# A planner's model of PSUM banks and of some durations, and a new set of its preferences, in a fused attention and feed-forward kernel

## The chip, the cores and the metric

The kernel runs on one core of one Trainium2 chip. The metric is the device time of one execution in microseconds (us), and the median of the runs is what counts. All arithmetic is in 32-bit floats. A core has a matrix engine (TensorE, PE in the profile), VectorE (DVE), ScalarE (ACT), GpSimd (POOL) and a queue that issues DMAs (SP). Matrix products land in PSUM, which has 8 banks of 2 KB in each of its 128 partitions. ACT and DVE read the banks.

## The reference, cut to what matters

Eight sequences `b`, each of 512 rows by 256 columns, go through the same three stages. The function `ffn` is two layers of windowed attention and a gated feed-forward; `ttt` is a sequential update of a matrix, row by row.

```
x = in_x                                      # (8, 512, 256)
x = x + 0.5 * ffn(layernorm(x))               # two layers
x = x + ttt(layernorm(x))
x = x + 0.5 * ffn(layernorm(x))               # the same two layers

ffn, one layer (8 heads of 64, window 128, hidden size 682):
  h = shift_token(x)                          # half of the columns come from the row before
  q, k, v = split(h @ wqkv)
  q, k = rotary(l2norm(q) * qs, l2norm(k) * ks)
  o = softmax(mask(q k^T * 8)) v              # a window sees itself and the one before
  x = x + o @ wo
  a, g = split(layernorm(shift_token(x)) @ w1 + b1)
  x = x + (a * gelu(g)) @ w2 + b2

ttt: z = layernorm(...) ; keys, queries, values = projections of z
  for each row t: y_t = W q_t ; W = W - 0.01 (W k_t - v_t) k_t^T
  result z + y
```

## The kernel before, in words

A sequence is cut into four windows of 128 rows (`NW`). The loops of `sequence` (one for each `b`) run over two halves, two layers, four windows, and in the attention over two groups of four heads. All weights stay in SBUF, so after the first loads the only DMAs are the load of a sequence, a second load of its input, and the store.

The program has no loops on the chip. While it is built, Python makes a list of *nodes*, each a small group of instructions on one engine, with its cost in nanoseconds, the nodes that it depends on, and the buffers that it takes and uses (`Node`, `Val`). `Scheduler.run` then goes through them as a list scheduler: it keeps a modelled clock for each engine, works out for each ready node the time `t` at which it could start, and emits the node with the smallest key. The key is that time, plus the cost of a change (of the shape class on PE, 100 ns; of the activation table on ACT, 1300 ns), minus the node's *preference*: the number of ns in the table `EARLY` under the node's name. A preference of 4700 lets a node go ahead of others whose time is up to 4.7 us earlier. The order in which nodes are emitted is the order of instructions on each engine, and it is all that the planner decides, apart from two choices: a copy out of PSUM may go to ACT or DVE, and some additions and multiplications to DVE or GpSimd. The waits between engines come from the framework, by the tiles that instructions touch, and not from the planner's clock.

Some costs and constants of the model: `HOP` is 60 ns from one engine to the next, `PE_TAIL` 170 ns more after TensorE, `T_TURN` the price of two 64-row transposes, `T_QUAD` and `T_QUADS` those of groups of 64x64 products. A buffer's slot comes free when the last node that uses its `Val` is ready. PSUM is the pool `"ps"` of eight banks; a node that needs a bank takes a `Val("ps")`.

Up to three sequences are in flight (the pool `lane`). `base` and `x` are their residual streams. In the attention of a window, in this order of data:

- `h.turn`, `h.copy` (L542, L506): x is transposed into `hT`.
- `qk` (L594): the products for k, then q, each 512 wide into one bank `pp`. From that bank ACT squares (`qk.square`, L613), and DVE multiplies with the rotary tables twice (`qk.straight` L638, `qk.swapped` L644). `qk.sum` (L620), `qk.add` (L650) and, on GpSimd, `qk.power` (L629, L630) and `k.scale` (L665) follow.
- `v` (L681): the product for v, and `v.copy` (L506).
- `qk.turn` (L704): 16 transposes put rotated k and q into two banks. `both_of` gives a view of both banks at once.
- `qk.copy` (L506), twice: the k half of that view to `kT`, the q half to `qT`, each 512 wide, each on ACT or DVE. Both read the same two banks.
- `sc` (L744): score products of 64x64 blocks from `kT` and `qT`, in two banks, for four heads. It depends on both copies and on `v`'s product.
- `least` (L787, DVE), `exp` (L799, ACT), `recip` (L813, DVE), `shares` (L820, DVE or GpSimd): the softmax.
- `pr.turn` (L846), `pr.copy` (L506), `po` (L883), `po.copy` (L506), `po.add` (L927): the weights are transposed and multiply v.
- `py` (L934), `x.attn` (L943): the output projection, added to x.

The feed-forward takes two windows at a time: `hs` (L972 to L975), `hs.stats`, `hn` (L996), `hn.turn` (L542), `h2T` (L1019), then `gate` and `value` (both L1041), `gelu` (L1063), `g` (L1082), `last` (L1041), `last.gelu` (L1102), `last.g` (L1116), and `down` (L1132), `remains` (L1143), `x.ffn` (L1154). The stage `ttt` solves the row recursion by blocks of 128 rows: products of 64x64 blocks at L1335, and the steps `pred`, `rest`, `u`, `y` (L1488, L1489) and `w` (L1500) window by window.

Nodes on PE have a class (`kind`): "full", "rows" (64-row transposes and others of less than 128 rows), "quad" (64x64 blocks) and "cols". A change of class is what the planner charges with 100 ns.

Of the kernel before, what the change touches and what calls it, by code (L numbers as in the profile page):

```python
# [15 lines left out]
B, S, D = 8, 512, 256  # L16
NW = S // P
HEADS, DH = 8, 64
# [3 lines left out]
NFC = HID // P  # L22
# [62 lines left out]

HOP = 60.0
PE_TAIL = 170.0
T_TURN = 58.0
T_QUAD = 116.0
T_QUADS = 224.0  # L90
T_BLOCKS = 450.0
# [4 lines left out]
def t_mm(n, times=1):  # L96
    return times * 2 * (n * 2 / 2.4 + 2.5)
# [14 lines left out]
def t_pool(n, spread=False):  # L112
# [2 lines left out]


EARLY = {
    "XT": -200,
    "_table": -250,
    "_turn": 250,  # L120
    "base.x": 300,
    "below": 5200,
    "block": 250,
    "bx": 400,
    "bx.copy": 100,
    "bx6": -150,
    "bx6.copy": 800,
    "cross.mask": -650,
    "down": -100,
    "edge": -550,  # L130
    "exp": -950,
    "g": 100,
    "gate": 5950,
    "gram": 250,
    "gram.copy": 2550,
    "h.copy": -250,
    "h.turn": 350,
    "h2T": -900,
    "hn": 250,
    "hn.turn": 250,  # L140
    "hs": 2000,
    "hs.rstd": -800,
    "hs.stats": 300,
    "k.scale": -500,
    "keys": 2350,
    "keys.copy": 500,
    "kq": 3450,
    "kq.copy": -450,
    "last": 400,
    "last.g": 300,  # L150
    "last.gelu": 250,
    "least": -250,
    "ones": -150,
    "po": 2000,
    "po.add": 5000,
    "po.copy": 200,
    "pr.copy": -150,
    "pr.turn": 250,
    "pred": 5000,
    "py": 50,  # L160
    "qk": 150,
    "qk.copy": 50,
    "qk.power": -1000,
    "qk.square": -750,
    "qk.sum": -500,
    "qk.swapped": 4700,
    "qk.turn": 1450,
    "recip": 3000,
    "remains": 1750,
    "rest": 1050,  # L170
    "sc": 4700,
    "start": 3050,
    "tv": 200,
    "tv.add": -1100,
    "u": 100,
    "u.copy": -100,
    "v.copy": 100,
    "value": 150,
    "w": 100,
    "w.add": -500,  # L180
    "x.ffn": -500,
    "x.rstd": -1250,
    "x.scale": 2500,
    "x.stats": -900,
    "xbx": 250,
    "xbx.t": 4750,
    "y": 2850,
    "z.stats": -1150,
    "zT": -1000,
    "zero": -2000,  # L190
    "zn.rstd": -2750,
    "zn.stats": -150,
    "zn.turn": 3000,
}


# [32 lines left out]
class Val:  # L229


    def __init__(self, tag):
        self.tag, self.users, self.slot, self.ap = tag, 0, None, None


class Node:
    def __init__(self, name, prio, eng, cost, emit, deps, takes, uses, kind, tail, port):
        self.name, self.early = name, EARLY.get(name, 0.0) - max(prio[0], 0) * EARLY.get("_seq", 0.0)
        self.prio, self.cost, self.emit, self.takes, self.kind = prio, cost, emit, takes, kind
        self.engs = eng if isinstance(eng, tuple) else (eng,)  # L240
        self.costs = cost if isinstance(cost, tuple) else (cost,)
        self.uses, self.next, self.ready, self.tail, self.port = uses, [], None, tail, port
        self.left = 0
        for d in deps:
            d.next.append(self)
            self.left += 1
        self.deps = deps
        for v in uses:
            v.users += 1


class Scheduler:
# [23 lines left out]
    def run(self):  # L276
        ready = [n for n in self.nodes if n.left == 0]
        left = len(self.nodes)
        while left:
            best = None  # L280
            for n in ready:
                room = self.room(n)
                if room is None:
                    continue
                at = max([room, *(d.ready for d in n.deps)])
                for eng, cost in zip(n.engs, n.costs):
                    t, turn = max(at, self.clock[eng], self.port if eng in n.port else 0.0), 0.0
                    if eng == "PE" and n.kind != self.pe_kind:
                        turn = PE_TURN
                    if eng == "ACT" and n.kind and n.kind != self.table:  # L290
                        turn = TABLE
                    more = EARLY.get(f"_{'table' if eng == 'ACT' else 'turn'}", 0.0) if turn else 0.0
                    key = (t + turn - n.early + more + (cost if len(n.engs) > 1 else 0.0), n.prio)
                    if best is None or key < best[0]:
                        best = (key, n, eng, cost, t, turn)
            assert best, f"no node can go: {left} left, " + str({k: len(v) for k, v in self.free.items()})
            _, n, eng, cost, t, turn = best
            ready.remove(n)
            left -= 1
            n.ran = eng  # L300
            self.turns[eng] = self.turns.get(eng, 0) + (turn > 0)
            for v in n.takes:
                slots = self.free[v.tag]
                v.slot = min(slots, key=lambda s: s[0])
                slots.remove(v.slot)
                v.ap = v.slot[1]
            n.emit(eng)
            end = self.gate.end(t + turn, cost) if eng == "PE" else t + turn + cost
            self.clock[eng] = end
            if eng in n.port:  # L310
                self.port = end
            if eng == "PE":
                self.pe_kind = n.kind
            if eng == "ACT" and n.kind:
                self.table = n.kind
            n.ready = end + n.tail + (PE_TAIL if eng == "PE" else 0.0)
            for v in n.uses:
                v.users -= 1
                if v.users == 0:
                    v.slot[0] = n.ready  # L320
                    self.free[v.tag].append(v.slot)
            for m in n.next:
                m.left -= 1
                if m.left == 0:
                    ready.append(m)
        return max(self.clock.values())
# [3 lines left out]
def macaron_kernel(ctx: ExitStack, tc: tile.TileContext, a: dict, out: bass.AP):  # L330
# [4 lines left out]
    ps = ctx.enter_context(tc.tile_pool(name="ps", bufs=1, space=bass.MemoryType.PSUM))  # L335
# [147 lines left out]
    def sequence(b):  # L483
# [6 lines left out]
        def pe(name, cost, emit, deps, takes=(), uses=(), kind="full"):  # L490
            return node(name, prio(), "PE", cost, lambda e: emit(), deps, takes, uses, kind)
# [54 lines left out]
        def attention(x, l, ready):  # L546

            wqkv, rt, wo, lnp, w1, b1, w2 = W[l]
            hT, kT, v, laid, vals, done = {}, {}, {}, {}, {}, []
            n_qk = n_v = n_k = None  # L550
            for w in range(NW):

                hT[w], pt = Val("hT"), Val("ps")
                n = transposes(
                    "h.turn",
                    lambda k, pt=pt: pt.ap[:, k * P : (k + 1) * P],
                    lambda k, w=w: x.ap[:, w, k * P : (k + 1) * P],
                    [ready[w], L["ident"]],
                    [pt, hT[w]],
                    [x],  # L560
                    2,
                )
# [11 lines left out]
                else:  # L574
# [7 lines left out]
                        uses=[hT[w], hT[w - 1]],  # L582
# [6 lines left out]
                for i in (1, 0):  # L589
                    pp, rot, tmp, st = Val("ps"), Val("rot"), Val("tmp"), Val("st")  # L590

                    def project(pp=pp, w=w, i=i):
# [14 lines left out]
                        takes=[pp, rot, tmp, st],  # L607
                        uses=[hT[w]],
# [6 lines left out]
                        uses=[pp, tmp],  # L615
# [8 lines left out]
                        uses=[tmp, st],  # L624
# [24 lines left out]
                    def add(e, rot=rot, tmp=tmp):  # L649
# [9 lines left out]
                        uses=[rot, tmp],  # L659
# [37 lines left out]
                def turn(pts=pts, turned=turned):  # L697
                    out = both_of(*pts)
                    for i in (1, 0):
                        rot = turned[i][0].ap  # L700
                        for g in range(HEADS // 2):
# [5 lines left out]

                n_k = pe(
                    "qk.turn",
                    HEADS * T_TURN,  # L710
                    turn,
                    [turned[0][1], turned[1][1], n_k],
                    takes=[*pts, kT[w], qT, oT],
                    uses=[turned[0][0], turned[1][0]],
                    kind="rows",
                )
                made = [
                    copy(
                        "qk.copy",
                        512,  # L720
                        lambda dst=dst: dst.ap.rearrange("p g (r t) -> p r g t", r=2),
                        lambda i=i, pts=pts: both_of(*pts)[:, :, i * 4 * DH : (i + 1) * 4 * DH].rearrange(
                            "p r (g t) -> p r g t", g=4
                        ),
                        [n_k],
# [11 lines left out]
                for g in range(2):  # L737

                    sc, prT = [Val("ps"), Val("ps")], Val("prT")
                    prs, sts = [Val("pr"), Val("pr")], [Val("s8"), Val("s8")]  # L740

                    def scores(sc=sc, g=g, w=w, qT=qT):
# [24 lines left out]

                    n_sc = pe(
                        "sc",
                        2 * (T_QUADS + (T_QUAD if w else 0.0)),  # L770
                        scores,
                        [made[1], n_v, *(laid[j] for j in blocks)],
                        takes=[*sc, *prs, *sts],
                        uses=[qT, *(kT[j] for j in blocks)],
                        kind="quad",
                    )
                    n_w = []
                    for par in range(2):
# [4 lines left out]
                        for k in range(2):  # L783
# [31 lines left out]
                            uses=[st],  # L815
                        )

                        def shares(e, st=st, par=par, prs=prs, nj=nj):
# [13 lines left out]
                                uses=[prs[par], st],  # L832
# [119 lines left out]
        def feed_forward(x, l, ready):  # L952
            wqkv, rt, wo, lnp, w1, b1, w2 = W[l]
            done = []
            for h in range(2):
# [188 lines left out]
                            pys[k].ap[:, 0:D], gT.ap[rows, rem], w2[rows, NFC, :], start=False, stop=True  # L1144
                        )

                n_d = pe("remains", t_mm(D) + 10, remains, [*downs, *made[NFC:]], uses=[*pys, gT], kind="rows")
                for k in range(2):

                    done.append(  # L1150
# [12 lines left out]
        def ttt(base, at):  # L1163
# [285 lines left out]
            for w in range(NW):  # L1449
# [36 lines left out]
                def outputs(w=w, U=U, pyy=pyy):  # L1486
# [3 lines left out]

                n_out = pe(
                    "y",
                    t_mm(D, 2 if w else 1), outputs, [n_uc, n_ca, n_wt], takes=[pyy], uses=[U, va, vb], kind="full"
                )
                if w < NW - 1:
                    pw = Val("ps")
# [160 lines left out]
```

## Time and profile before

| what | value |
|---|---|
| median of 3 runs | 2931.66 us (2930.18 to 2934.65) |
| the profiled execution | 2928.53 us |
| its span, first to last instruction | 2926.8 us |
| TensorE busy, granted clock | 2794.0 us (95%), 0.997 |
| VectorE, ScalarE, GpSimd busy | 1968.5 (67%), 1630.8 (56%), 1294.0 us (44%) |
| chain that ended last | PE 88%, DVE 5%, ACT 4%, POOL 2%, issue 1% |
| DMA | 27.96 MB in all, mean 10 GB/s |

A row of the groups reads: line, engine, operation, output and inputs by the program's names, shape, count; then busy us and mean ns of one; then the idle time of the engine just before these instructions, and what ended most of it. "ps" is any PSUM bank. Weight loads (PEld) overlap the matmuls. In the table of waits a row reads: who waited, for whom, us in total, times, the longest in us. In the timeline: start and length in us, engine, line, operation, count, and in brackets the idle time before it and its releaser.

### The profile page before, as it was taken

How to read it: one execution, taken by the hardware profiler on the slowest of the kernel's cores; microseconds unless marked ns; L12 is line 12 of the kernel's file. 1: busy time of each engine (PE TensorE's matmuls, PEld its weight loads, DVE VectorE, ACT ScalarE, POOL GpSimd, SP SyncE). 2: the span in 40 equal slices, each digit the busy share in tenths (PEclk: the TensorE clock that was granted, in tenths of full speed). 3: DMA queues.
4: the chain of work that ended last, by engine and by line, in shares of the span. 5: the costliest groups of instructions: out<-in, count | busy, mean ns of one | idle time of the engine just before them, and what ended most of it. 6: DMA issues, size and time to landing. Idle time of an engine off the chain costs nothing.

```text
span 2926.8 us, 75703 instructions
## 1 busy us (share of the span) xinstructions
PE 2794.0 (95%) x30448; PEld 2057.5 (70%) x30448; DVE 1968.5 (67%) x6125; ACT 1630.8 (56%) x4328; POOL 1294.0 (44%) x1844
## 2 busy tenths in 40 slices
PE   7999999999999999999999999999999999999997
PEld 4776776776767767677676776767766677676666
DVE  6777666666776666766677666766666666666664
ACT  4655655555566555565555655555455654645553
POOL 5444453544455244452445524454244542444432
PEclk9999999999999999999999999999999999999999
DMA  5000000000000000000000000000000000000000
GB/s 181 2 2 2 2 2 1 2 2 2 23 2 2 2 16 9 2 2 2 20 5 2 2 1 23 2 1 2 1 23 2 2 2 1 16 2 2 9 2 8
DMA packets 20615, 27.96 MB, mean 10 GB/s; under 512 B 2172, under 2 KB 17704, under 8 KB 20264
## 3 DMA queue, kind: packets, MB, share of 16 engines
q1 hardware_dynamic: 20264, 23.12, 2.4%
q8 instruction: 239, 3.92, 0.6%
q14 instruction: 112, 0.92, 0.1%
HBM read 18.93 MB, written 4.19 MB: 8 GB/s over the span
## 4 chain that ended last, share of the span: by engine, by line
PE 88%; DVE 5%; ACT 4%; POOL 2%; issue 1%; DMA 0%; SPq 0%; ACTq 0%; DVEq 0%; POOLq 0%
PE ps L1041 20%; PE ps L594 15%; PE ps L1132 9%; PE ps L934 7%; PE ps L681 7%; PE ps L744 6%; PE ps L883 6%; PE ps L846 4%; PE ps L704 2%; PE ps L542 2%; PE ps L1335 2%; ACT kT L506 1%; PE ps L1143 1%; DVE qT L506 1%; PE ps L972 1%
## 5 line engine op out<-in xcount | busy, mean ns | idle before, releaser
L1041 PE MATMUL ps<-h2T,w 128*128 128x256 f32 (+1 forms) x2816 | 656.1, 383 | 5.0 <-ACT kT L506 2.2
L1041 PEld LDWEIGHTS ps<-h2T,w 128*128 128x128 f32 (+1 forms) x2816 | 520.4, 189 | 109.6 <-issue 21.5
L820 POOL TENSOR_TENSOR pr<-pr,s 128x384 f32<-128x384 f32 (+1 forms) x304 | 240.7, 796 | 649.4 <-DVE s L813 619.3
L594 PE MATMUL ps<-wqkv,hT 128*128 128x512 f32 x1024 | 495.4, 609 | 3.0 <-ACT prT L506 1.3
L799 ACT ACTIVATE pr<-pr,s 128x192 f32<-128x192 f32 (+1 forms) x1024 | 440.5, 433 | 30.7 <-DVE s L787 28.6
L630 POOL TENSOR_TENSOR st<-st,powc 128x8 f32<-128x8 f32 x256 | 433.0, 1691 | 21.3
L787 DVE CUSTOM_DVE_ANT_0 pr<-ps,amask,st 128x192 f32<-128x192 f32 (+1 forms) x1024 | 360.8, 394 | 54.4 <-PE ps L744 52.2
L613 ACT ACTIVATE tmp<-ps 128x512 f32<-128x512 f32 x256 | 153.4, 599 | 290.7 <-DVE rot L638 266.4
L1132 PE MATMUL ps<-w,gT 128*128 128x256 f32 x1280 | 296.6, 382 | 2.1 <-ACT kT L506 1.1
L594 PEld LDWEIGHTS ps<-wqkv,hT 128*128 128x128 f32 x1024 | 184.5, 192 | 152.6 <-issue 136.0
L506 ACT COPY prT<-ps 128x512 f32<-128x512 f32 (+1 forms) x453 | 220.6, 544 | 117.1 <-PE ps L846 106.7
L1132 PEld LDWEIGHTS ps<-w,gT 128*128 128x128 f32 x1280 | 239.6, 190 | 48.0 <-issue 10.0
L744 PE MATMUL ps<-kT,qT 64*64 64x128 f32 (+1 forms) x7168 | 190.8, 251 | 73.5 <-DVE qT L506 37.3
L744 PEld LDWEIGHTS ps<-kT,qT 64*64 64x64 f32 x7168 | 167.6, 133 | 127.2 <-ACT qT L506 55.9
L638 DVE TENSOR_TENSOR rot<-ps,rt 128x512 f32<-128x512 f32 x256 | 175.9, 687 | 120.1 <-PE ps L594 108.8
L934 PE MATMUL ps<-wo,oT 128*128 128x256 f32 x1024 | 243.9, 381 | 0.2 <-DVE oT L927 0.2
L681 PE MATMUL ps<-wqkv,hT 128*128 128x512 f32 x512 | 242.8, 599 | 1.2 <-ACT kT L506 1.2
L629 POOL TENSOR_SCALAR st<-st 128x8 f32<-128x8 f32 x256 | 67.2, 262 | 375.3 <-DVE st L620 371.9
L934 PEld LDWEIGHTS ps<-wo,oT 128*128 128x128 f32 x1024 | 191.6, 190 | 48.4 <-issue 19.9
L883 PEld LDWEIGHTS ps<-prT,v 64*64 64x64 f32 x7168 | 173.8, 133 | 61.7 <-issue 23.0
L1082 DVE SCALAR_TENSOR_TENSOR gT<-ps,b,gl 128x256 f32<-128x256 f32 x320 | 148.7, 481 | 100.2 <-PE ps L1041 59.9
L883 PE MATMUL ps<-prT,v 64*64 64x64 f32 (+1 forms) x7168 | 206.6, 249 | 6.2 <-ACT prT L506 5.3
(127 smaller groups left out, 4488.5 us busy)
## 6 DMA issues: line engine op xcount, KB each, us to landing
x<-in_x_dram SPq DMA_DIRECT2D x8, 512.0 KB, 5.4
base<-in_x_dram SPq DMA_DIRECT2D x8, 512.0 KB, 3.8
out_dram<-base SPq DMA_DIRECT2D x8, 512.0 KB, 3.3
w<-in_w_dram SPq DMA_DIRECT2D x6, 640.0 KB, 8.0
wqkv<-in_wqkv_dram SPq DMA_DIRECT2D x2, 1024.0 KB, 7.2
wqkv<-in_wqkv_dram SPq DMA_DIRECT2D x2, 512.0 KB
wo<-in_wo_dram SPq DMA_DIRECT2D x2, 512.0 KB
gT<-in_rope_dram SPq DMA_DIRECT2D x1, 512.0 KB
```

Of the source, the lines that this page charges most:

```text
L506: (nc.scalar.copy if e == "ACT" else nc.vector.tensor_copy)(dst(), src())
L594: nc.tensor.matmul(pp.ap, hT[w].ap[:, c * P : (c + 1) * P], wqkv[:, c, i * INNER : (i + 1) * INNER], start=(c == 0), stop=(c == 1),)
L630: nc.gpsimd.tensor_tensor(ss, ss, powc[:, 0:HEADS], ALU.pow)
L681: nc.tensor.matmul(pv.ap, hT[w].ap[:, c * P : (c + 1) * P], wqkv[:, c, 2 * INNER : 3 * INNER], start=(c == 0), stop=(c == 1),)
L744: nc.tensor.matmul(sc[par].ap[half(c), k * 4 * DH + at : k * 4 * DH + at + keys.stop - keys.start], qT.ap[half(par), 2 * g + k, half(c)], ...
L787: nc.vector.tensor_tensor_reduce(out=pr(k, nj), in0=sc.ap[:, k * 4 * DH : k * 4 * DH + nj], in1=amask[:, 0:nj] if w else amask[:, 3 * DH : ...
L799: nc.scalar.activation(pr(k, nj), pr(k, nj), AF.Exp, bias=st.ap[:, k : k + 1], scale=-1.0, accum_out=st.ap[:, 2 + k : 3 + k],)
L820: (nc.vector if e == "DVE" else nc.gpsimd).tensor_tensor(both, both, st.ap[:, 4:6].unsqueeze(2).to_broadcast([P, 2, nj]), ALU.mult)
L883: nc.tensor.matmul(po[r].ap[half(par), k * P + first : k * P + first + cols * DH], v[j].ap[half(r), hd * DH : (hd + 1) * DH], prT.ap[half( ...
L934: nc.tensor.matmul(py.ap[:, 0:D], oT.ap[:, c, :], wo[:, c, :], start=(c == 0), stop=(c == INNER // P - 1))
L1041: nc.tensor.matmul(dst.ap[0:rows, 0 : 2 * P], w1[:, kc, col : col + rows], h2T.ap[:, kc, :], start=(kc == 0), stop=(kc == 1),)
L1132: nc.tensor.matmul(py.ap[:, 0:D], gT.ap[:, at : at + P], w2[:, c, :], start=(c == 0), stop=False)
```

## The change

It touches the planner alone: no instruction of the program is added, removed or altered, and only their order can differ, with the choice of engine where there is one. It has three parts.

Banks: each `Val` remembers which engine used it last and until when (`last`). A node that uses a PSUM bank may not start, on the modelled clock, before the last user has ended, if that was on another engine. The rule goes by the banks that a node itself takes or uses.

Durations: `T_TURN` goes from 58 to 62 ns; `qk.turn` gets 50 ns more, `sc` 38, `remains` 94, and `y` 200 where it has two products (w > 0).

Preferences: nearly all of `EARLY` is replaced. Of some 70 entries the lines below show those that the text speaks of and the largest moves.

```diff
-T_TURN = 58.0
+T_TURN = 62.0
...
 EARLY = {
-    "_table": -250,
+    "_table": -500,
     "_turn": 250,
...
-    "below": 5200,
+    "below": -1200,
...
-    "bx6": -150,
+    "bx6": 5050,
...
-    "gate": 5950,
+    "gate": 4800,
...
-    "po": 2000,
-    "po.add": 5000,
+    "po": 3450,
+    "po.add": 500,
...
     "qk.copy": 50,
...
-    "qk.swapped": 4700,
-    "qk.turn": 1450,
+    "qk.swapped": 1600,
+    "qk.turn": 1100,
...
-    "sc": 4700,
-    "start": 3050,
+    "sc": 3850,
+    "start": 5350,
...
+    "v": -50,
...
 class Val:
         self.tag, self.users, self.slot, self.ap = tag, 0, None, None
+        self.last = None
...
 class Node:
+        self.banks = [v for v in self.uses if v.tag == "ps"]
...
 class Scheduler, run:
                     t, turn = max(at, self.clock[eng], self.port if eng in n.port else 0.0), 0.0
+
+                    t = max([t, *(v.last[1] for v in n.banks if v.last and v.last[0] != eng)])
...
             n.ready = end + n.tail + (PE_TAIL if eng == "PE" else 0.0)
+            for v in n.banks:
+                v.last = (eng, n.ready)
...
                 n_k = pe(
                     "qk.turn",
-                    HEADS * T_TURN,
+                    HEADS * T_TURN + 50.0,
...
                         "sc",
-                        2 * (T_QUADS + (T_QUAD if w else 0.0)),
+                        2 * (T_QUADS + (T_QUAD if w else 0.0)) + 38.0,
...
-                n_d = pe("remains", t_mm(D) + 10, remains, [*downs, *made[NFC:]], uses=[*pys, gT], kind="rows")
+                n_d = pe("remains", t_mm(D) + 104.0, remains, [*downs, *made[NFC:]], uses=[*pys, gT], kind="rows")
...
                     "y",
-                    t_mm(D, 2 if w else 1), outputs, [n_uc, n_ca, n_wt], takes=[pyy], uses=[U, va, vb], kind="full"
+                    t_mm(D) if w == 0 else t_mm(D, 2) + 200.0,
+                    outputs, [n_uc, n_ca, n_wt], takes=[pyy], uses=[U, va, vb], kind="full"
```

More of the change, by code (lines that the diff above doesn't have):

```diff
@@ L117 @@
 EARLY = {
-    "XT": -200,
-    "_table": -250,
+    "XT": 400,
+    "XT6": -250,
+    "_table": -500,
     "_turn": 250,
-    "base.x": 300,
-    "below": 5200,
-    "block": 250,
-    "bx": 400,
-    "bx.copy": 100,
-    "bx6": -150,
-    "bx6.copy": 800,
-    "cross.mask": -650,
+    "base.x": 3000,
+    "base.y": -750,
+    "base.z": -1250,
+    "below": -1200,
+    "block": -500,
+    "bx": 450,
+    "bx6": 5050,
+    "cross.mask": 1400,
     "down": -100,
-    "edge": -550,
+    "edge": -50,
@@ L131 @@
     "exp": -950,
     "g": 100,
-    "gate": 5950,
-    "gram": 250,
-    "gram.copy": 2550,
+    "gate": 4800,
+    "gelu": -550,
     "h.copy": -250,
[L137 to L151, printed above, removed]
+    "h.turn": 200,
+    "h2T": -700,
+    "hn.turn": 200,
@@ L152 @@
+    "hs.rstd": -850,
+    "hs.stats": 400,
+    "keys": 1550,
+    "keys.copy": -1000,
+    "kq": 1850,
+    "kq.copy": -500,
+    "last": 1300,
+    "last.g": -200,
+    "last.gelu": 300,
     "least": -250,
-    "ones": -150,
-    "po": 2000,
-    "po.add": 5000,
+    "po": 3450,
+    "po.add": 500,
     "po.copy": 200,
-    "pr.copy": -150,
+    "pr.copy": -100,
     "pr.turn": 250,
-    "pred": 5000,
-    "py": 50,
+    "pred": 3100,
     "qk": 150,
     "qk.copy": 50,
-    "qk.power": -1000,
@@ L164 @@
-    "qk.square": -750,
+    "qk.power": -1250,
+    "qk.square": -600,
     "qk.sum": -500,
-    "qk.swapped": 4700,
-    "qk.turn": 1450,
-    "recip": 3000,
-    "remains": 1750,
-    "rest": 1050,
-    "sc": 4700,
-    "start": 3050,
[L173 to L177, printed above, removed]
-    "value": 150,
[L179 to L186, printed above, removed]
@@ L187 @@
-    "y": 2850,
-    "z.stats": -1150,
-    "zT": -1000,
+    "qk.swapped": 1600,
+    "qk.turn": 1100,
+    "recip": 700,
+    "remains": 1250,
+    "rest": 2800,
+    "sc": 3850,
+    "start": 5350,
+    "tv": 2000,
+    "tv.add": -900,
+    "u.copy": 400,
+    "v": -50,
+    "value": 150,
+    "w.add": -400,
+    "x.attn": -100,
+    "x.ffn": -700,
+    "x.rstd": -1400,
+    "x.scale": 200,
+    "x.stats": 100,
+    "xbx": 1200,
+    "xbx.t": 800,
+    "y": 550,
+    "z.rstd": 1700,
+    "z.scale": 4250,
@@ L190 @@
+    "z.stats": 2350,
+    "zT": -1700,
     "zero": -2000,
-    "zn.rstd": -2750,
-    "zn.stats": -150,
-    "zn.turn": 3000,
+    "zn.rstd": -2850,
+    "zn.scale": 2000,
+    "zn.turn": 4450,
 }
```

## The prediction, made before the result was known

> **What bounds the kernel now.** I read the page first: busy time by engine, then the slices.
>
> ```profile
> span 2926.8 us, 75703 instructions
> PE 2794.0 (95%) x30448; PEld 2057.5 (70%) x30448; DVE 1968.5 (67%) x6125; ACT 1630.8 (56%) x4328; POOL 1294.0 (44%) x1844
> ...
> PEclk9999999999999999999999999999999999999999
> ```
>
> TensorE is at work 95% of the span at full clock; no other engine passes 70%. The change adds and removes no instruction, so it can only take time from the 2926.8 - 2794.0 = 132.8 us in which TensorE stands still, and a little from how its work is ordered. Where those lie, the view by windows tells (length, then PE busy):
>
> ```profile
> 0.00:25.00 25.00, 16.96 (x60) 7.59 (x64) 12.88 (x26) 6.45 (x12) 17.23 (x39) 1.00 0.94 322
> ...
> 100.00:2700.00 2600.00, 2508.34 (x27621) 1857.30 (x27620) 1768.48 (x5519) 1472.38 (x3909) 1167.72 (x1661) 1.00 0.02 5
> ...
> 2850.00:2926.80 76.80, 61.21 (x631) 47.20 (x630) 38.19 (x112) 29.72 (x74) 18.76 (x25) 0.96 0.02 8
> ```
>
> Start (8.0 us) and end (15.6) are the load of the first weights and the dependent chain of the last sequence; no order removes them. 91.7 us lie in the steady middle. Who waits there, from the groups by line (last columns: idle before, releaser) and the table of waits:
>
> ```profile
> L744 PE MATMUL ps<-kT,qT 64*64 64x128 f32 (+1 forms) x7168 | 190.8, 251 | 73.5 <-DVE qT L506 37.3 <-ACT qT L506 35.7 <-ACT hT L506 0.4
> L542 PE MATMUL ps<-sq,x 128*128 128x128 f32 x256 | 48.3, 289 | 18.3 <-DVE x L533 10.0 <-DVE x L1154 4.6 <-DVE tmp L644 2.8
> L883 PE MATMUL ps<-prT,v 64*64 64x64 f32 (+1 forms) x7168 | 206.6, 249 | 6.2 <-ACT prT L506 5.3 <-DVE gT L1116 0.3
> ...
> ACT tmp L613 <- DVE rot L638: 266.4, 203, 3.6
> ...
> DVE qT L506 <- ACT kT L506: 72.0, 49, 3.4
> ```
>
> One place holds 73.5 of it: the score products (L744, node "sc") wait for the copies of q and k out of PSUM (L506, "qk.copy"), in 81 stalls of 0.9 us. The two lower lines are the bank: the DVE copy of qT waits for the ACT copy of kT from the same two banks, and the square on ACT (L613) waits for DVE's product (L638) in the same bank. The timeline shows one stall:
>
> ```profile
> 228.44 0.66 PE L704 MATMUL ps<-sq,rot 64*128 64x64 f32 x16
> ...
> 229.32 0.90 PE L883 MATMUL ps<-prT,v 64*64 64x128 f32 x32 [0.22 <-ACT prT L506]
> 230.29 0.58 ACT L506 COPY kT<-ps 128x512 f32<-128x512 f32 x1 [1.02 <-PE ps L883]
> ...
> 230.90 0.69 DVE L506 COPY qT<-ps 128x512 f32<-128x512 f32 x1 [1.97 <-ACT kT L506]
> ...
> 231.65 1.57 PE L744 MATMUL ps<-kT,qT 64*64 64x128 f32 x64 [1.43 <-DVE qT L506]
> ```
>
> Two delays add up. The copies run one after the other (230.29 to 231.59), which the planner doesn't know. And the first copy starts 1.2 us after its transposes (L704) end at 229.10: it was released by L883, a *later* product that it doesn't read. Pairing the start times of all 128 copy pairs: in 66 the first copy was released by a TensorE instruction later than its transposes, on average 1.0 us (ACT, then DVE) to 1.8 us (both on ACT) after them; these 66 pairs hold 59.3 of the stall. The change doesn't tell the planner of this second delay.
>
> **What the Trainium skill says.** "PSUM — Partial Sum Buffer", section on bank collisions: no two of TensorE, ScalarE and VectorE may touch one bank in the same partitions at once, reads against reads included, and a back end puts a dependency between them. The trace agrees: where ACT copies first and DVE second, DVE starts 33 ns (median) after ACT ends. "Perfetto Trace Analysis", on the most-contended engine, warns that matmul busy time misjudges TensorE, since matmuls are pipelined; so I also take starts: a 128x256 matmul follows another after 216 ns, though its row shows 383. "TensorEngine Tiling (Array Packing)", Key Properties: changing the tiling mode drains TensorE. Here 309 ns instead of 216 pass before a 64x64 product that follows such a matmul, about 93 ns for each of 993 changes of shape class, 92 us. "ScalarE: Activation LUTs", on table loads, gives 1283 ns a load; the trace has 1283.
>
> **The change, part by part**, against the profiled execution (2928.53 us; its span 2926.8 and 1.7 around it). The median of the runs is 2931.66, 3.1 more.
>
> *Bank rule at the copies.* In 55 pairs ACT copies first and DVE second, in 5 the reverse, in 68 both are on ACT. The planner so far takes DVE beside ACT as free: ready after about 0.7 us of copying. With the rule DVE would start behind ACT's 0.59 and one hop and take 0.69, so ACT twice (1.17) is the earlier end, and most pairs go to ACT. By start times and idle in the trace, the 60 mixed pairs hold 39.9 us of the stall and the 68 ACT pairs 33.0, or 0.49 each. If the mixed pairs come to 0.49: 60 x 0.49 = 29, **-11 us**. ACT takes over some 45 copies x 0.59 = 27 us, at 56% busy; DVE loses 31.
>
> *Bank rule at the square.* ACT stands 266.4 us in 203 waits behind L638, with its queue (copies, exps, gelus) behind it. That is no TensorE time in itself, but the planner thinks those followers earlier than they are. With the rule it puts one ahead. In ACT pairs the second copy starts on average 0.7 us after the first has ended, other work being between. I take a third of the 35.7 us that L744 waits for ACT's qT: **-12 us**. Bounds: 0, and all of the 35.7.
>
> *Durations.* qk.turn 8x4+50 = 82 ns x128; pr.turn 16 ns x64 and 32 x192; sc 38 x256; remains 94 x64; y 200 x24: 10.5+7.2+9.7+6.0+4.8 = 38 us of TensorE work that the planner did not count. They agree with the trace (16 transposes of L704 take 553 ns to the next start; 8x58 = 464, new 546). No instruction becomes shorter; the plan of buffers and waits fits better. Idle in the middle outside L744 is 91.7 - 73.5, about 18 us, some of L744's being in the last 227; I take a third, **-6 us**; bounds +10 and -15.
>
> *Preferences.* No direct price. They move whole nodes, and nothing but the first loads, one base reload a sequence and one store waits on a DMA; SP's queue is never what TensorE waits for after 10 us. The penalty for a change of shape class (_turn) stays 250; I take 0, with 5% of 993 x 0.093, 5 us, either way. The penalty for a table load falls from -250 to -500: more of them are possible, see below.
>
> Sum: 2928.5 - 11 - 12 - 6 = 2899.5; plus 3.1: **2903 us**, 1.0% faster. What is late next is the same L744, still 45 us or so, behind copies that wait for later products.
>
> **The rivals.** *B: the stall mostly goes.* The planner sees the copies end half a microsecond later and puts the v product (four matmuls of 429 ns, 1.7 us) between; then even falsely released copies (1.0 to 1.8 us late) are covered. For it: at 95% busy there is always other work of the three sequences in flight. Against: the ACT pairs were already planned serially and still stall. Three quarters of 73.5, 55, less at the same -6 and some hidden drain: 2931.7 - 55 = 2877.
>
> *C: it doesn't do what it says.* The later products are what decides, the copies wait for them as before, and the retuned order brings no more than noise: 2930.
>
> *D: slower, by ACT.* The copies go to ACT and so does a keener change of table. Now there are 78+74+5 = 157 loads of 1.28 us. A load ahead of a copy or an exp delays TensorE by up to 1.28 us, or nothing. With half reaching TensorE, 60 more loads cost 60 x 0.64 = 38; from 29/0.64 = 45 more loads they eat my gain. At 60 with the gain at the square gone too (12): 2903 + 38 + 12 = 2953; as ACT is idle 44% I take it a little milder: 2945.
>
> **How the numbers follow.** My forecast has 0.53, B 0.21, C 0.12, D 0.14. A measurement of this kernel can tell 0.2% (6 us) from no change. Forecast and B are faster; of C a third is faster (0.04) and two thirds the same (0.08); D is slower. So faster 0.78, same 0.08, slower 0.14. My own bounds (square 0 to -35.7, other idle +10 to -15, classes 5) give 2870 to 2931; B's centre is 2877 and its better half reaches 2862; at the top C's 2930 and its noise to 2934. That leaves out D and the best of B, under 2 in 10.
>
> **What would show it.** Right: qT copies on DVE fall from 55 to under 20; the wait of DVE's qT for ACT's kT falls from 72.0 below 25; the wait of the square for L638 falls well below 266.4; L744's idle falls to 40 to 55 us; first copies are still often released by a later product. B is right if L744's idle is below 25. D is right if table loads exceed 200 and PE idle rises at L883 and L846. I am wrong if PE's idle stays at 130 (C), or if the gain comes with PE busy below 2780, which would mean fewer class changes rather than fewer waits.

## The result and the profile after

The changed kernel takes 2897.58 us (median; 2897.02 to 2898.26) where the one before takes 2933.15 beside it. The ratio is 0.9879, 95% interval 0.9862 to 0.9896: 1.2% faster, 35.6 us. Predicted were 2903 us and 28.7 us less. The profiled execution of the kernel before was one of its fastest (2928.53 us), so the two profiles lie only some 30 us apart. Of the reasons that the prediction gave, one holds by itself in a run, and it is worth a third of the gain (11.7 us); most of the rest hangs on a wait that the prediction saw and put aside.

The page of the changed kernel (the lines of its code that the text speaks of are numbered 2 higher than before; busy us by engine):

```profile
span 2896.4 us, 75802 instructions
PE 2792.6 (96%) x30448; PEld 2063.2 (71%) x30448; DVE 1966.6 (68%) x6110; ACT 1638.9 (57%) x4317; POOL 1331.6 (46%) x1884
```

TensorE's busy time has not moved (2794.0 before, a difference of 1.4). Its idle time, span less busy, fell from 132.8 to 103.8 us; 29.0 + 1.4 is the 30.4 by which the span is shorter. From the groups by line, the three places that matter (last columns: idle before, releaser), and from the table of waits the square:

```profile
L746 PE MATMUL ps<-kT,qT 64*64 64x128 f32 (+1 forms) x7168 | 195.6, 255 | 36.4 <-ACT qT L508 32.4 <-DVE qT L508 3.7
L885 PE MATMUL ps<-prT,v 64*64 64x128 f32 (+1 forms) x7168 | 204.5, 249 | 13.0 <-ACT prT L508 9.9 <-DVE prT L508 1.2 <-DVE s L789 1.0
L544 PE MATMUL ps<-sq,x 128*128 128x128 f32 x256 | 46.8, 286 | 10.5 <-DVE x L535 10.5
...
ACT tmp L615 <- DVE rot L640: 162.3, 144, 3.5
```

The scores (L746) stand idle for 36.4 us instead of 73.5, that is 37.1 less; everywhere else together it is 67.4 instead of 59.3, 8 more. And most of the copies of qT that were on DVE have moved to ACT, as the groups by shape show, on ACT, then on DVE:

```profile
L508 ACT COPY qT<-ps 128x512 f32<-128x512 f32 x115 | 67.8, 590 | 64.4 <-PE ps L596 28.6 <-PE ps L1043 10.4 <-DVE row L1469 5.6
L508 ACT COPY kT<-ps 128x512 f32<-128x512 f32 x115 | 67.3, 586 | 236.7 <-PE ps L848 86.7 <-PE ps L706 63.4 <-PE ps L596 38.5
```

```profile
L508 DVE COPY qT<-ps 128x512 f32<-128x512 f32 x13 | 8.9, 688 | 11.3 <-PE ps L885 5.5 <-PE ps L1337 3.3 <-PE ps L1043 1.3
```

Of the q copies 13 are on DVE, 55 before, and DVE's wait for ACT's copy of kT, 72.0 us before, isn't among the first three here: it is under 1.3. But the second line still says what the prediction called a second delay: the copy of kT is released by transposes of other data (L848, 86.7 us) more than by its own (L706, 63.4). Paired by start times (the first copy of a pair is the one that starts earlier), 74 of the 128 first copies are now released by a later product, 66 before, and those pairs hold 31.6 of the 36.4 us. What became of the stall is that the scores come later: the median time from the end of both copies to the start of the scores went from 55 ns, which is no room at all, to 374.

### The profile page after: what moved, and what is told of

It is laid out like the page before. It is cut to its first block, busy times and chain, and to the rows that moved or that the text cites. A ratio compares the mean times of both kernels' runs of the same rounds, so it can differ in the third digit from the quotient of the medians.

```text
span 2896.4 us, 75802 instructions
## 1 busy us (share of the span) xinstructions
PE 2792.6 (96%) x30448; PEld 2063.2 (71%) x30448; DVE 1966.6 (68%) x6110; ACT 1638.9 (57%) x4317; POOL 1331.6 (46%) x1884
## 4 chain that ended last, share of the span: by engine, by line
PE 91%; DVE 3%; ACT 3%; POOL 2%; issue 1%; DMA 0%; SPq 0%; DVEq 0%; POOLq 0%; ACTq 0%
PE ps L1043 21%; PE ps L596 16%; PE ps L1134 9%; PE ps L936 8%; PE ps L683 7%; PE ps L885 6%; PE ps L746 6%; PE ps L848 4%; PE ps L706 2%; PE ps L544 2%; PE ps L1337 2%; PE ps L1145 1%; PE ps L1257 1%; PE ps L974 1%; ACT qT L508 1%
## 5 line engine op out<-in xcount | busy, mean ns | idle before, releaser
L822 POOL TENSOR_TENSOR pr<-pr,s 128x384 f32<-128x384 f32 (+1 forms) x345 | 271.5, 794 | 480.4 <-DVE s L815 476.7
L801 ACT ACTIVATE pr<-pr,s 128x192 f32<-128x192 f32 (+1 forms) x1024 | 441.2, 434 | 57.9 <-DVE s L789 54.4
L615 ACT ACTIVATE tmp<-ps 128x512 f32<-128x512 f32 x256 | 153.1, 598 | 186.9 <-DVE rot L640 162.3
L508 ACT COPY prT<-ps 128x512 f32<-128x512 f32 (+1 forms) x397 | 193.8, 543 | 105.2 <-PE ps L848 99.9
L746 PEld LDWEIGHTS ps<-kT,qT 64*64 64x64 f32 x7168 | 172.1, 136 | 104.5 <-ACT qT L508 58.5
L746 PE MATMUL ps<-kT,qT 64*64 64x128 f32 (+1 forms) x7168 | 195.6, 255 | 36.4 <-ACT qT L508 32.4
L885 PE MATMUL ps<-prT,v 64*64 64x128 f32 (+1 forms) x7168 | 204.5, 249 | 13.0 <-ACT prT L508 9.9
L1065 ACT ACTIVATE gl<-ps,b 128x256 f32<-128x256 f32 x320 | 140.1, 473 | 118.5 <-PE ps L1043 113.1
```

Source lines behind the costliest of these rows:

```text
L508: (nc.scalar.copy if e == "ACT" else nc.vector.tensor_copy)(dst(), src())
L746: nc.tensor.matmul(sc[par].ap[half(c), k * 4 * DH + at : k * 4 * DH + at + keys.stop - keys.start], qT.ap[half(par), 2 * g + k, half(c)], ...
L801: nc.scalar.activation(pr(k, nj), pr(k, nj), AF.Exp, bias=st.ap[:, k : k + 1], scale=-1.0, accum_out=st.ap[:, 2 + k : 3 + k],)
L822: (nc.vector if e == "DVE" else nc.gpsimd).tensor_tensor(both, both, st.ap[:, 4:6].unsqueeze(2).to_broadcast([P, 2, nj]), ALU.mult)
L885: nc.tensor.matmul(po[r].ap[half(par), k * P + first : k * P + first + cols * DH], v[j].ap[half(r), hd * DH : (hd + 1) * DH], prT.ap[half( ...
```

## The experiments

"Close banks" below is the edit that turned out to matter most. The copies read both banks of a pair through one strided view (`both_of`: from the lower bank to the higher, with a step). If the framework takes such a view to touch the banks in between, a copy waits for any product that was emitted earlier into one of these. In the order of the changed program this holds for 75 of the 128 first copies; 74 of them are exactly those that the trace shows released by a later product, and of the other 53 none is. Before, it is 78, of which 66. In the kernel before, where nothing lay between, a first copy began a median of 42 ns after its transposes ended; where something did, 1039.

**Close banks in the changed kernel and in the kernel before.** When `qk.turn` takes its two banks, it takes those of the free ones that lie closest. No node moves and no engine changes; only bank numbers differ.

```diff
+            near = None
+            if n.name == "qk.turn":
+                open_ = [s for s in self.free["ps"] if s[0] <= t]
+                near = min(
+                    ((p, q) for p in open_ for q in open_ if p[3] < q[3]), key=lambda s: (s[1][3] - s[0][3], s[0][0] + s[1][0])
+                )
             for v in n.takes:
                 slots = self.free[v.tag]
                 v.slot = min(slots, key=lambda s: s[0])
+                if near and v.tag == "ps":
+                    v.slot, near = near[0], near[1:]
```

In the changed kernel: 

> The changed kernel; the only difference is which two banks the transposes of q and k take: of the banks that are free at that time, the two closest. The order of all nodes and their engines stay exactly the same; the copy's view spans 1 bank of distance in 206 of 256 copies instead of 70. If copies wait for later TensorE work because their view spans the banks between, first copies released by a later product fall from 74 to about 15, L746's idle falls from 36.4 to about 10, and the time by some 22 us to 2875. If they are late for another reason (ACT's queue, semaphores shared by nodes), nothing moves: 2897.

Measured: 2840.26 us, ratio to before 0.9691 (0.9678 to 0.9704). It is 57 us faster than the changed kernel, two and a half times what was expected. At the scores it went as expected: 15 first copies are still released by a later product, and the idle time is 8.9 us. The rest went at other places: TensorE's idle time outside the scores fell from 67.4 to 50.3 us, its busy time by 11.6. Part of this looks like the same wait the other way round: ahead of other products than the scores, none of which reads kT or qT, TensorE stood idle for 9.8 us until a copy of kT or qT was done, and now for 0.6.

In the kernel before: 

> The kernel before with the same choice of close banks and nothing else; order and engines are those of before. If spanned banks cause the late first copies, released by later products in 66 pairs that hold 59.3 us of the stall, L744's idle falls from 73.5 to about 25, what is left being the mixed pairs that still copy one after the other, and the time to about 2885. If the taking of turns by ACT and DVE is what stalls the scores, it stays above 60 and the time above 2920.

Measured: 2845.77 us, ratio 0.9715 (0.9702 to 0.9728). The kernel before, with other bank numbers and nothing else, beats the changed kernel by 52 us. Of its first copies 5 are released by a later product, 66 before. The stall that the prediction showed at 228.44 us can be found again in its timeline, the same instructions in the same order:

```profile
220.67 0.66 PE L712 MATMUL ps<-sq,rot 64*128 64x64 f32 x16
...
221.38 0.60 ACT L514 COPY kT<-ps 128x512 f32<-128x512 f32 x1
221.55 0.90 PE L891 MATMUL ps<-prT,v 64*64 64x128 f32 x32 [0.22 <-ACT prT L514]
...
222.02 0.69 DVE L514 COPY qT<-ps 128x512 f32<-128x512 f32 x1 [0.86 <-ACT kT L514]
...
222.76 1.57 PE L752 MATMUL ps<-kT,qT 64*64 64x128 f32 x64 [0.32 <-DVE qT L514]
```

The first copy begins 0.05 us after its transposes end, beside the product that it used to wait for, and TensorE stands idle for 0.32 us instead of 1.43. What is left is the taking of turns, and this run prices it: the groups by line of this kernel, and of the changed one with close banks, have for the scores

```profile
L752 PE MATMUL ps<-kT,qT 64*64 64x128 f32 (+1 forms) x7168 | 192.6, 252 | 19.1 <-DVE qT L514 17.6 <-ACT qT L514 1.1 <-ACT hT L514 0.4
```

```profile
L754 PE MATMUL ps<-kT,qT 64*64 64x128 f32 (+1 forms) x7168 | 193.1, 252 | 8.9 <-ACT qT L516 8.5 <-DVE qT L516 0.3
```

So of 73.5 us of stall before, 54 belonged to the spanned banks and 19 to all else. TensorE's busy time fell as well, from 2794.0 to 2781.1. Start by start, outside the stretches in which the profile of either run grants TensorE half the clock (19 us before, 13 here), the scores follow the instruction before them 58.8 us sooner in sum, and their idle time fell by 54.4: the part of a stall that lies under the modelled end of the matmul before it is not idle time in the profile. Of the 12.9 us, 3.4 lie in the stretches at half clock and are not the waits'. The two plans, 35.6 us apart, are 5.5 apart with close banks.

**All copies on ACT, in the order of before.** The planner's choice of engine is overridden when the copy is emitted.

```diff
             def emit(e):
+                e = {"qk.copy": "ACT"}.get(name, e)
                 (nc.scalar.copy if e == "ACT" else nc.vector.tensor_copy)(dst(), src())
```

> The kernel before with its order untouched, but every copy of q and k is put on ACT where the planner had given 60 of the 256 to DVE. This is the first term of the prediction by itself: the mixed pairs no longer take turns. Expected by it: 11 us less, 2921, with L744's idle near 62. If moving copies to ACT is the larger part of the change's gain: 2905 or less. If ACT, whose queue is served in order, pays for the 60 copies: 2931 or more.

Measured: 2920.25 us, 11.7 less than the 2931.9 beside it, ratio 0.9955 (0.9943 to 0.9968). The scores' idle is 63.6. The first term of the prediction, 11 us, is right in this order.

**The q copies on DVE, in the order of after.** The reverse: in the changed kernel k goes to ACT and q to DVE whatever the planner says (an argument `on` of `copy` does it).

> The changed kernel with its order untouched, but every copy of k is put on ACT and every copy of q on DVE, the planner unaware of it, so that nearly all 128 pairs take turns at their banks across the two engines. If the engine is what the change gained by, 110 pairs lose 0.2 us or more each: 2920. If the change gained by planning the scores later, so that they have room (374 ns in the median between the end of the copies and the scores), most of it is absorbed: at most 8 us more, 2905, and L746's idle stays under 46.

Measured: 2928.09 us, 30.5 more than the changed kernel. The room did not absorb it; that expectation fell. The scores' idle rose by 16.8 to 53.2 us.

```profile
L748 PE MATMUL ps<-kT,qT 64*64 64x128 f32 (+1 forms) x7168 | 195.6, 255 | 53.2 <-DVE qT L509 52.7
L509 DVE COPY qT<-ps 128x512 f32<-128x512 f32 x128 | 88.2, 689 | 148.5 <-ACT kT L509 62.1 <-PE ps L597 40.4 <-PE ps L1339 14.0
```

The planner had not reckoned with the copies there. The second copy began 0.80 us after the end of the first on average, not the 33 ns of a bare turn: in 53 pairs DVE stood ready and began 0.09 us after it, in 41 it was still at other work (0.95 us), and in 34 it stood idle until a later product of TensorE released it (1.74 us), as with a late first copy.

**The bank rule, and the rule with the durations, under the old preferences.** Kernel before plus the lines of `Val.last`; changed kernel with the old table `EARLY`.

Rule alone: 

> The bank rule alone is put into the kernel before; its durations and preferences stay. If the rule itself brings the gain, by planning the square and the second copy later, this runs near the changed kernel: about 2905 us, with L744's idle near 40. If the gain needs preferences that were found with the rule, the old ones are out of tune with it: slower than before, 2945 us or more, with TensorE's idle above the 133 us of before and spread over other lines than L744.

Rule and durations: 

> The changed kernel with the old preferences: bank rule and durations, without the new table. If the model is what counts, about 2900 us. If model and preferences belong together, slower than before, 2945 us or more, much like the run with the bank rule alone. If the durations by themselves matter, this differs from that run by more than 10 us.

Measured: 3025.5 us (ratio 1.032, 1.0306 to 1.0334) and 3013.69 us (1.0287, 1.0273 to 1.0301). The rule alone does shorten the stall of the scores, as the first of these lines shows, and gives back more elsewhere: TensorE is idle for 163.4 us (3022.8 less 2859.4) and busy 65 us longer. About half of the 65 are the clock. It was granted 0.985 here (0.984 to 0.988 in the four runs) and 0.997 in the profile of before: TensorE was busy for 79 us at half the clock, before for 15, and half of the 64 more is 32. Another 13 us, at the prediction's 93 ns, are 141 more changes of shape class (1134, before 993).

```profile
L750 PE MATMUL ps<-kT,qT 64*64 64x128 f32 (+1 forms) x7168 | 195.6, 254 | 46.6 <-ACT qT L512 37.6 <-DVE qT L512 7.2 <-DVE gT L1122 0.7
L889 PE MATMUL ps<-prT,v 64*64 64x128 f32 (+1 forms) x7168 | 214.8, 252 | 31.9 <-ACT prT L512 27.0 <-DVE kT L512 1.4 <-ACT oT L512 1.2
L852 PE MATMUL ps<-sq,pr 64*128 64x64 f32 x3584 | 158.3, 228 | 12.8 <-POOL pr L826 7.0 <-DVE pr L826 5.6
```

Preferences are offsets in ns against one model's clock, and the old ones did not carry over to the new model. The new table can't be tried without the rule either: the planner then comes to a point at which no node can go.

**Parts of the rule, each with preferences found anew for it.** The line `self.banks` is limited by the node's name: to the copies of q and k, or to all others. The durations are the old ones.

```diff
-        self.banks = [v for v in self.uses if v.tag == "ps"]
+        self.banks = [v for v in self.uses if v.tag == "ps" and name == "qk.copy"]
```

Copies alone: 

> The kernel before with the bank rule for the copies of q and k alone (all other nodes ignore it), old durations, and preferences found anew for this rule. If the rule at these copies is what brings the gain, because it makes the planner leave room ahead of the scores, L744's idle falls from 73.5 to about 40 and the time to 2900. By the prediction's first term it is worth 11 us: 2920. If it is the durations or the square that count: no faster than 2928.

All others alone (`!=`): 

> The reverse: the bank rule for all nodes but the copies of q and k (so for the square behind DVE's product), old durations, preferences found anew for this rule. By the prediction's second term: 12 us less, 2919, the ACT wait for L638 well below 266. If ACT has enough idle time that its waits at the square cost TensorE nothing: within 6 us of before, L744's idle near 73.

The whole rule without the durations: 

> The change without its durations: bank rule as in the changed kernel, old durations, preferences found anew for this. By the third term of the prediction the durations are worth 6 us: 2904. If they are worth as much as the other two terms leave of the whole (35.6 - 11.7 - 14.2, 10 us): 2908. If they are worth nothing, 2898 or less.

Measured: copies alone 2930.77 us (ratio 0.9999, 0.9991 to 1.0007); all others 2917.73 (0.9948, 0.9935 to 0.9962), with ACT's wait for L638's counterpart at 159.7 us and the scores' idle at 63.5; the whole rule without durations 2940.55 (1.0033, 1.002 to 1.0045). They don't add up to the whole. In the first the scores' idle fell to 48.6 us, 25 less, and TensorE lost it again elsewhere: its idle time is 127.1 (2929.0 less 2801.9), its busy time 8 us up. The preferences of these three runs come from short searches, with another start than those of the changed kernel, so a loss here may be the search's; only the gain of the second stands, and the next run is on that.

**The rule for all others, with close banks.** The same edit as above in that kernel.

> The kernel with the bank rule for all nodes but the copies of q and k, now with close banks and nothing else changed. It asks whether its 14 us are worth of the planned square. If so they stay when the copies are no longer late: 2846 - 14 = 2832. If its plan merely lay better around the late copies, they go: 2843 or more.

Measured: 2840.82 us, ratio 0.9692 (0.9678 to 0.9705). Its 14 us shrink to 5 against the 2845.8 of before with close banks, and the intervals overlap at the edge. The 5 are a net figure: this plan changes the shape class 1068 times, 75 more than the order of before.

**Close banks and all copies on ACT, in the order of before.**

> The kernel before with its order untouched, close banks for the transposes of q and k, and all copies of q and k on ACT: both delays ahead of the scores are taken away without any better plan. If the two are independent: 2846 less the 13 us that the mixed pairs still held with close banks, 2833, with L744's idle under 8; then the changed kernel's plan is worth nothing once the waits are gone (2840 with close banks). If ACT's queue or the plan matters too: 2840 or more.

Measured: 2839.37 us, ratio 0.9689 (0.9676 to 0.9703); 6.4 less than close banks alone, not 13, and the scores' idle is 11.0, not under 8. With close banks the mixed pairs whose first copy was on time (ACT, then DVE) still held 13 us of the scores' idle; about half of that was in reach. The order of before, untouched, is now level with the changed kernel's plan.

| plan | as it is | close banks |
|---|---|---|
| before | 2931.9 | 2845.8 |
| before, copies on ACT | 2920.3 | 2839.4 |
| rule for all but the copies | 2917.7 | 2840.8 |
| changed kernel | 2897.6 | 2840.3 |

**The changed planner, close banks, preferences found anew.** Other nodes leave neighbouring free banks alone, too.

```diff
+            if eng == "PE":
+                open_ = [s for s in self.free["ps"] if s[0] <= t]
+                at_ = {s[3] for s in self.free["ps"]}
...
+                else:
+                    near = sorted(open_, key=lambda s: ((s[3] - 1 in at_) + (s[3] + 1 in at_), s[0]))
```

> The changed kernel's bank rule and durations, close banks for the transposes (other nodes leave neighbouring free banks alone, too), and preferences found anew by a longer search. 252 of 256 copies read neighbouring banks. If the planner now describes the chip well, a plan that it holds 30 us shorter comes out shorter by most of that than the changed kernel with close banks: 2815 to 2825. If its remaining errors are as large as that: 2840 or more.

Measured: 2817.57 us, ratio 0.9612 (0.9599 to 0.9626): 3.9% faster than before and 80 us faster than the changed kernel. The scores hardly wait any more. Of TensorE's idle time 46 us are left of a span of 2817.6: 9 in the first 25 us, 8 in the next 75, 16 in the 2600 after that and 13 in the last 118. What the 22.7 us against the changed kernel with close banks are due to is not taken apart: 252 instead of 206 of the 256 copies read neighbouring banks, the shape class changes 921 times instead of 979, and there are 141 table loads instead of 171.

```profile
PE 2771.4 (98%) x30448; PEld 2058.4 (73%) x30448; DVE 1985.8 (70%) x6138; ACT 1582.9 (56%) x4252; POOL 1338.1 (47%) x1891
...
L772 PE MATMUL ps<-kT,qT 64*64 64x128 f32 (+1 forms) x7168 | 190.6, 252 | 1.5 <-ACT qT L534 1.3
```

## Why the prediction was right, and where its steps failed

The time, the sign and the place were right: the idle time that went is the scores'. Forecast were 40 to 55 us of it left; measured are 36.4, somewhat less. That the sum came out so near has luck in it: the scores gave 37 us where some 28 were forecast, and elsewhere 8 us were lost where 6 were to be won. Two slips in the working changed nothing: the 68 ACT pairs hold 33.6 us of the stall, not 33.0, and the bounds of 2870 to 2931 leave out the 5 us for class changes that they name.

*Bank rule at the copies, -11.* Right, and by its mechanism: the copies went to ACT (13 q copies left on DVE, under 20 forecast), and the engine alone, in the old order, gives 11.7. The size belongs to that order: with close banks it is 6.4, and taken back in the changed order it costs 30.5.

*Bank rule at the square, -12.* ACT's wait fell as forecast, from 266.4 to 162.3 us, and a planner that knows of all turns but the copies' gains 14.2. But this is not what the term said, that ACT's followers come in time: with close banks some 5 of the 14 remain. The rest went when the copies were no longer late: it hung on them, and the term doesn't know of that.

*Durations, -6.* Not shown. With the old preferences they are worth 11.8 us on top of the rule (3025.5 to 3013.7); the rule without them, its preferences found anew, is 43 us slower than the changed kernel. The searches differ, so no size can be given. Idle time outside the scores rose by 8 us where a fall of 6 was forecast: that step failed.

*Preferences, 0.* Failed as an account. They are not a part with a price of zero but the thing that carries the rest: with the rule and the old table the kernel is 3% slower.

*What is late next: the same scores, behind copies that wait for later products.* Right, and larger than I took it for. I saw that 66 pairs were released by a product that they don't read and left it as a fact that the change doesn't touch. It was the cause of 54 of the 73.5 us. The changed kernel does not remove it. It gains, beyond the 11.7 us of the engine, because its plan leaves more room ahead of the scores and so covers part of the late copies. With close banks, where few copies are late, the median room is 1.26 us in its order and 1.04 in the order of before with the copies on ACT. And take the lateness away, and the four rows of the table lie within 6.4 us of each other, three of them within 1.5. B's mechanism, room that covers late copies, was therefore at work as much as my forecast's own; I set its time too low because I expected it all or not at all.

*D, slower by ACT.* Table loads rose from 157 to 85+69+17 = 171, a third of the 45 at which it would have decided. TensorE's idle time at L883 did rise, from 6.2 to 13.0 us, that at L846 fell from 3.7 to 1.9. Changes of shape class went from 993 to 979.

Why the framework lets the strided view reach over the banks between was not looked into; that the distance of the banks is what decides is shown by the runs in which nothing else differs.

## What to carry to other kernels

When an instruction is released by one whose data it doesn't touch, find out why before planning around it: here the buffer numbers alone were worth 86 us, the planner's new model and preferences 36, and only 5 of these on top. Give buffers that are read through one view neighbouring places. A planner's preferences belong to its model: compare models only with preferences found for each.

## What was not expected of the hardware

TensorE's busy time fell by 13 us when only bank numbers were changed (2794.0 to 2781.1, the same 30448 matmuls), some 3 of them by the clock and the rest by shorter waits, so the 132.8 us of idle time understated the waits. And one engine change in the same order can cost far more than the instruction: 115 q copies moved from ACT's 590 ns to DVE's 689, with 13 k copies moved to ACT, cost 30.5 us, about 0.27 us for each of the 115 where the durations differ by 0.1.
